# A four-layer graph network on one core: layer-0 scores by symmetry, layer 1 by seven products, and a plan with two times per layer

## The chip, the cores and the metric

The kernel runs on one core of a Trainium2 chip. The metric is the device time in microseconds of one execution; three runs of the kernel before gave 2713.51, 2717.15 and 2717.57 us, so the median is 2717.15 us. The core has five engines with instruction queues of their own: TensorE (PE in the profile, its weight loads PEld), VectorE (DVE), ScalarE (ACT), GpSimd (POOL) and SyncE (SP, which here issues transfers only). They meet through semaphores.

## The reference

The input is 128 graphs of 128 nodes with 256 features, in fp32, and an integer adjacency of 128x128 per graph. Four layers follow each other, and each is wrapped as `x = layernorm(x + layer(x))`:

```python
# layer 0: four scores by edge type, masked, softmax
e_k = leaky_relu(einsum('bid,bjd->bij', hidden * a_k, hidden))   # k = 0..3
alpha = where(adj == k + 1, e_k, ...);  out = softmax(alpha) @ hidden
# layer 1: message sum, mean by in-degree, relu
h = x @ W_msg; msg = einsum('bij,biu->bju', adj, h) / max(deg, 1)
out = relu(x @ W_upd + msg + bias)
# layer 2: three GRU steps with aggregation over adj != 0
m = h @ weight[i]; aggr = einsum('bst,bsd->btd', A, m); h = gru_cell(aggr, h)
# layer 3: graph attention
e = leaky_relu(f_i + f_j), masked by adj > 0; out = elu(softmax(e) @ (h @ W))
```

Two facts are used below. The score of layer 0 before its mask, `(h * a_k) h^T`, is symmetric in i and j. And layer 1 multiplies the same `x` by two square matrices, `W_upd` and `W_msg`, which the kernel holds side by side in `w_um`.

## The kernel before

Graphs go in 32 groups of four (`G = 4`). One group passes `loading`, `layer0`, `layer1`, three `step`s of `gru`, and `layer3`. Features lie in two chunks of 128 (`KC = 2`). Some six groups are in flight at a time.

Nothing is issued while the layers' functions run. Each call is recorded as an `Op` (class at line 156) with the buffers that it reads and writes; every call goes through line 232, so the profile gives nearly all instructions that line, and they are told apart by tile names. At the end a list scheduler (from line 1010 on) walks through a simulated time, in which each engine takes, among the operations that could start, the one with the smallest nominal time, and issues it. That fixes the order of every queue. Nominal times come from `paced(stage, part, g)` at line 338: all operations recorded since the last call are spread evenly, by cost, between two times of the table `TIMES`, moved by `g * PERIOD` and, for the first and last six groups, by the tables `HEAD` and `TAIL`. Durations in the simulation come from cost functions at lines 251 to 287, such as this one for TensorE:

```python
took = 0.11 if op == "transpose" else 0.056 if split else 0.005 + m_of(out[0]) / 600.0
```

Tiles with the same tag share a fixed number of buffers (`hT` has 8, `xb` 2, `xs` 2, `z` 4, PSUM banks `ps` 4 and `gate` 4). For some groups a tag borrows the memory of another (`LENT`, line 973).

**Layer 0** (line 604). `xT` holds the four graphs' features turned over. For each of the four edge types, `prepared(k)` makes a mask `mk` on POOL and two scaled copies `xs` on ACT. TensorE then fills one bank of 512 columns: per graph and feature chunk one matmul, with `xT` as stationary and 128 columns of `xs` moving. DVE copies the bank into `alpha` where the mask is set. Softmax, the product with `x_in`, the residual and the norm follow; the result `xa` is turned over through DRAM into `x1T`.

**Layer 1** (line 669). Per graph, TensorE multiplies `x1T` with all 512 columns of `w_um`, two matmuls. ACT copies the message half into `hu`, whose last column is 1 for the degree, set each time by a POOL memset; DVE adds the bias to the update half. Then one product with the adjacency per graph gives message sums and degree.

**Gates of the GRU** (line 767) already use a scheme of seven products in place of eight. Four 256-column halves live in two banks, and a running sum in `shared` is copied out ("snapshot") at three points between products, each of which makes TensorE wait for the copy before it may add to that bank again. The scheme's sums of inputs are made in `sums`, those of the weights in `weights`.

**Transfers.** A 128x128 turn is a DVE transpose of 32x32 blocks into `z`, a write to DRAM (`way`), and four reads back (`back`, line 506), all issued by SP in order.

Of the kernel before, what the change touches and what calls it, by code (L numbers as in the profile page):

```python
# [8 lines left out]
F32 = mybir.dt.float32  # L9
U8 = mybir.dt.uint8  # L10
# [3 lines left out]
OP = mybir.AluOpType  # L14
# [4 lines left out]
def kernel(  # L19
# [223 lines left out]
    def service(out, ins):  # L243

        tag = out[0].buf.tag if out else "out"
        return 1.5 if tag == "out" else SERVED.get(tag, 0.82 if tag[:3] == "way" else 0.5)
# [39 lines left out]
    def sp_cost(op, n, out, ins, pointers, sums):  # L286
# [10 lines left out]
    PERIOD = 81.73028  # L297
    EAGER, RUSH = 4.9441, 1.5064
    HOP, PE_HOP, SLACK, DMA_SLACK = 0.0975, 0.1022, 0.2622, 0.8243
    STAGES = ("loading", "layer0", "layer1", "step0", "step1", "step2", "layer3")  # L300
    TIMES = {
        "weights": ((-80.6792, -53.8982), (-234.5413, -66.3537), (-85.3398, -177.0436), (-97.3878, -222.0278), (-90.3491, -54.1657), (-171.8955, -44.6841), (-116.1849, 18.7475),),
        "loading": ((-270.5681, -253.3431), (-73.2168, -291.6634),),
        "layer0": ((-167.8607, -107.2636),),
        "layer1": ((-55.0836, 1.9826),),
        "step0": ((-0.0120, 6.9518), (0.2402, 27.6105), (15.5871, 41.1624),),
        "step1": ((50.3003, 61.9650), (57.0688, 76.7749), (63.5441, 96.9672),),
        "step2": ((105.0974, 124.9583), (122.1936, 130.3892), (118.2271, 151.0122),),
        "layer3": ((180.2686, 241.7351),),
    }  # L310
    HEAD = (
        (-8.812, -175.978, -47.271, -14.819, 0.990, 29.605, 4.780),
        (9.303, 38.059, -27.415, 8.695, 4.650, -13.814, 31.463),
        (-161.158, -14.643, 11.133, 0.523, -1.844, 22.264, 10.467),
        (-173.643, 45.499, 14.505, 11.786, 0.810, 10.190, -5.124),
        (-171.750, -3.449, 12.137, -8.917, 5.023, 2.080, 7.957),
        (-245.977, -21.192, 24.177, 5.969, 4.162, 11.377, 24.028),
    )
    TAIL = (
        (127.197, -10.789, 1.076, -13.469, 10.703, 11.032, 13.210),  # L320
        (17.815, -18.016, -1.019, -11.707, 1.115, -15.520, -14.882),
        (80.227, -2.934, 25.075, -16.097, -14.182, 5.595, 38.386),
        (92.761, -52.578, -27.642, -24.660, -19.396, -6.316, 54.637),
        (216.288, -67.705, -36.885, -29.712, 25.798, 36.675, 75.653),
        (364.741, 17.401, 10.112, 11.988, 17.448, 68.637, 12.013),
# [36 lines left out]
    neg_half = tile_of("neg_half", [P, G])  # L362
    acol = tile_of("acol", [P, 4, KC])
# [10 lines left out]

    w_sh = tile_of("w_sh", [P, 3, 3, P])
    w_sm = tile_of("w_sm", [P, NL, 3, 3, P])

    def weights():
# [3 lines left out]
        for src, tag, bufs in ((w_ih, "hT", 8), (w_hh, "rest", 4)):  # L382
# [45 lines left out]
        for i in range(NL):  # L428
            wT = tile_of("hT", [P, KC, D], 8)
# [40 lines left out]


# [132 lines left out]
    def layer0(g, s):  # L604
# [12 lines left out]
        def prepared(k):  # L617
            mk = tile_of("mk", [P, G, N], 2, U8)
            POOL.tensor_scalar(mk, a_f, float(k + 1), None, op0=OP.is_equal)
            xs = []  # L620
            for c in range(KC):
                t = tile_of("xs", [P, T], 2)
                ACT.mul(t, xT[c], acol[:, k, c : c + 1])
                xs.append(t)
            return mk, xs

        ready = [prepared(0)]
        for k in range(4):
            if k < 3:
                ready.append(prepared(k + 1))  # L630
            mk, xs = ready.pop(0)
            ps = bank()
            with PE:
                PE.needs(mk)
                for b in range(G):
                    cols = slice(b * N, (b + 1) * N)
                    for c in range(KC):
                        PE.matmul(ps[:, cols], xT[c][:, cols], xs[c][:, cols], start=(c == 0), stop=(c == KC - 1))
            DVE.copy_predicated(alpha.rearrange(FLAT), mk.rearrange(FLAT), ps)

        leaky(alpha, alpha, 0.0)
        pT, rinv = softmax(alpha, "0", g == 0)
# [26 lines left out]
    def layer1(g, s):  # L669
# [5 lines left out]
        DVE.tensor_scalar(s.a_ne, a_f, 0.0, None, op0=OP.not_equal)  # L675
        hu = []
        for b in range(G):
            hu.append(tile_of("hu", [P, 2 * D + 1], 2))
            POOL.memset(hu[b][:, 2 * D :], 1.0)
            ps = bank()  # L680
            with PE:
                for c in range(KC):
                    PE.matmul(ps, xT[:, b, c, :], w_um[:, c, :], start=(c == 0), stop=(c == KC - 1))
            ACT.copy(hu[b][:, D : 2 * D], ps[:, D:])
            DVE.tensor_add(hu[b][:, :D], ps[:, :D], bias_row)
        res = tile_of("xb", [P, G, D], 2)
# [18 lines left out]
        for c in range(KC):  # L705
            t = tile_of("hT", [P, T], 8)
# [12 lines left out]
    def gru(g, s):  # L719
# [5 lines left out]
        def step(i, hT, parts):  # L725
# [107 lines left out]
            def update(c, z, n, d):  # L833

                DVE.scalar_tensor_tensor(d, z, 1.0, d, op0=OP.add, op1=OP.mult)
                new[c] = n if last_step else tile_of("hT", [P, T], 8)
# [56 lines left out]
    def layer3(g, s, first, last):  # L893
# [50 lines left out]

        res = tile("xd", [P, n, D])
        ninv = tile_of(f"ninv_{three}", [P, n], 2)
        DVE.tensor_scalar_mul(ninv, rinv, -1.0)
        for h in range(n // 2):
# [27 lines left out]
            "probT_0": ("probT_3", 1), "x1T": ("xd", 1), "xs": ("rT", 2),  # L976
        },
        NG - 2: {"xc": ("xa", 2), "rT": ("xT", 2)},
        NG - 1: {
            "q": ("x_in", 1), "t_r": ("x_blocks", 1), "t_i": ("xb", 2), "t_z": ("xb", 2),  # L980
            "xc": ("xa", 2), "rT": ("xs", 2),
        },
    }
# [150 lines left out]
```

## Time and profile before

| What | Value |
|---|---|
| Median of three runs | 2717.15 us |
| The profiled execution | 2713.67 us |
| Its span, first to last instruction | 2711.9 us |
| Mean granted TensorE clock | 0.997 |
| PE busy | 2663.1 us (98%) |
| PE weight loads busy | 2232.4 us (82%) |
| DVE busy | 2187.9 us (81%) |
| ACT busy | 1806.7 us (67%) |
| POOL busy | 1596.5 us (59%) |
| DMA packets | 1317391, 286.89 MB |
| Share of 16 DMA engines, main queue | 50.7% |

An fp32 matmul shows as two records (two matmul records and two weight loads), a bf16 one as one. In the groups by line, layer 0's products `ps<-xs,xT` have 1984 records, layer 1's `ps<-w_um,x1T` 496, and the gates 8064; a few records of layers 0 and 1 stand under other names where a tag borrows memory. Matmul records overlap, since the end of one is modelled past the start of the next; the pace is read from starts. The busy share is an average over stages. `L232` is the recording helper's line, common to nearly all instructions.

### The profile page before, as it was taken

How to read it: one execution, taken by the hardware profiler on the slowest of the kernel's cores; microseconds unless marked ns; L12 is line 12 of the kernel's file. 1: busy time of each engine (PE TensorE's matmuls, PEld its weight loads, DVE VectorE, ACT ScalarE, POOL GpSimd, SP SyncE). 2: the span in 40 equal slices, each digit the busy share in tenths (PEclk: the TensorE clock that was granted, in tenths of full speed). 3: DMA queues.
4: the chain of work that ended last, by engine and by line, in shares of the span. 5: the costliest groups of instructions: out<-in, count | busy, mean ns of one | idle time of the engine just before them, and what ended most of it. 6: DMA issues, size and time to landing. Idle time of an engine off the chain costs nothing.

```text
span 2711.9 us, 45196 instructions
## 1 busy us (share of the span) xinstructions
PE 2663.1 (98%) x14340; PEld 2232.4 (82%) x14340; DVE 2187.9 (81%) x5058; ACT 1806.7 (67%) x4330; POOL 1596.5 (59%) x1538
## 2 busy tenths in 40 slices
PE   8999999999999999999999999999999999999996
PEld 6788888888887888888888888888888888888785
DVE  5777888778788887788887888887888888878877
ACT  4556776666776666766667766767767666667666
POOL 4554576654666555666556665556575555665552
PEclk9999999999999999999999999999999999999999
DMA  5535645554555455555555555555555556435441
GB/s 130 106 78 102 126 91 123 108 104 97 114 113 114 98 121 102 110 113 117 101 117 104 106 117 112 110 113 103 107 116 107 114 113 125 97 75 105 90 86 47
DMA packets 1317391, 286.89 MB, mean 106 GB/s; under 512 B 1068192, under 2 KB 1313056, under 8 KB 1317152
## 3 DMA queue, kind: packets, MB, share of 16 engines
q1 hardware_dynamic: 1314704, 281.63, 50.7%
q8 instruction: 115, 1.88, 0.3%
q10 hardware_dynamic: 2448, 2.36, 0.3%
q14 instruction: 124, 1.02, 0.1%
HBM read 168.44 MB, written 115.41 MB: 105 GB/s over the span
## 4 chain that ended last, share of the span: by engine, by line
PE 85%; DVE 9%; ACT 2%; DMA 2%; issue 1%; SPq 1%; POOL 0%; POOLq 0%; DVEq 0%; ACTq 0%
PE gate L232 58%; PE ps L232 27%; DVE z L232 1%; DVE xb L232 1%; DVE st L232 1%; DVE t_d L232 1%; SPq L232 1%; DVE rest L232 1%; DMA e<-way_f 1%; DVE t_m L232 1%; DVE t_r L232 0%; DVE xa L232 0%; DVE hT L232 0%; DMA hn<-way_h 0%; DVE t_z L232 0%
## 5 line engine op out<-in xcount | busy, mean ns | idle before, releaser
L232 POOL TENSOR_TENSOR t_r<-t_r,t_i 128x512 f32<-128x512 f32 x186 | 244.5, 1322 | 248.9 <-ACT t_i L232 164.4
L232 PE MATMUL gate<-t_h,w_hhT 128*128 128x256 f32 x1152 | 345.8, 383 | 5.1 <-ACT xb L232 2.5
L232 PE MATMUL gate<-t_m,w_sm 128*128 128x256 f32 x1152 | 342.4, 380 | 1.1 <-DVE t_m L232 0.8
L232 PE MATMUL gate<-t_m,c_gi 128*128 128x256 f32 x1152 | 341.8, 379 | 0.0
L232 PE MATMUL gate<-t_h,w_sh 128*128 128x256 f32 x1152 | 339.5, 382 | 1.8 <-ACT q L232 0.9
L232 PE MATMUL gate<-agT,c_gi 128*128 128x256 f32 x1152 | 336.1, 380 | 0.7 <-ACT t_r L232 0.6
L232 PE MATMUL gate<-hT,w_hhT 128*128 128x256 f32 x1152 | 333.7, 381 | 0.2 <-PE gate L232 0.2
L232 POOL TENSOR_TENSOR t_d<-hT,t_n 128x512 f32<-128x512 f32 x192 | 257.3, 1348 | 32.6 <-ACT t_n L232 32.1
L232 POOL TENSOR_TENSOR rstd<-rstd,neg_half 128x4 f32<-128x4 f32 x128 | 147.7, 1154 | 197.6 <-DVE rstd L232 124.7
L232 PEld LDWEIGHTS gate<-t_h,w_hhT 128*128 128x128 f32 x1152 | 208.9, 190 | 60.4 <-issue 23.2
L232 PEld LDWEIGHTS gate<-t_h,w_sh 128*128 128x128 f32 x1152 | 212.3, 190 | 54.3 <-issue 16.7
L232 PEld LDWEIGHTS ps<-xs,xT 128*128 128x128 f32 x1984 | 242.0, 193 | 12.5 <-issue 2.2
L232 PE MATMUL ps<-xs,xT 128*128 128x128 f32 x1984 | 244.2, 276 | 2.6 <-DVE xa L232 1.4
L232 PEld LDWEIGHTS gate<-t_m,w_sm 128*128 128x128 f32 x1152 | 217.1, 190 | 34.1 <-DVE t_m L232 2.2
L232 PEld LDWEIGHTS gate<-agT,c_gi 128*128 128x128 f32 x1152 | 216.8, 190 | 31.8 <-ACT t_r L232 1.2
L232 PEld LDWEIGHTS gate<-t_m,c_gi 128*128 128x128 f32 x1152 | 218.0, 190 | 30.2 <-ACT t_i L232 0.2
L232 PEld LDWEIGHTS gate<-hT,w_hhT 128*128 128x128 f32 x1152 | 214.2, 190 | 30.8 <-issue 2.9
L232 PE MATMUL ps<-w_um,x1T 128*128 128x512 f32 x496 | 232.7, 593 | 1.1 <-ACT x1T L232 1.1
L232 ACT ACTIVATE q<-gate,bhn 128x256 f32<-128x256 f32 x372 | 177.0, 476 | 81.3 <-PE gate L232 77.0
L232 POOL TENSOR_SCALAR mk<-a_f 128x512 uint8<-128x512 f32 x128 | 212.3, 1665 | 20.7 <-DVE alpha L232 13.2
L232 POOL MEMSET alpha<- 128x512 f32 (+1 forms) x63 | 33.1, 525 | 314.0 <-DVE z L232 277.8
L232 ACT ACTIVATE xs<-xT,acol 128x512 f32<-128x512 f32 x248 | 173.2, 719 | 41.2 <-PE ps L232 30.6
(231 smaller groups left out, 6668.0 us busy)
## 6 DMA issues: line engine op xcount, KB each, us to landing
way<-z SPq DMA_DIRECT2D x188, 256.0 KB, 2.4
way_h<-z SPq DMA_DIRECT2D x126, 256.0 KB, 2.4
hn<-way_h SPq DMA_DIRECT2D x504, 64.0 KB, 2.5
x_blocks<-in_x_dram SPq DMA_DIRECT2D x248, 64.0 KB, 2.5
x_in<-in_x_dram SPq DMA_DIRECT2D x31, 512.0 KB, 4.2
way_p<-z SPq DMA_DIRECT2D x62, 256.0 KB, 2.5
probT<-way_p SPq DMA_DIRECT2D x248, 64.0 KB, 2.8
hT<-way SPq DMA_DIRECT2D x248, 64.0 KB, 2.5
```

Of the source, the lines that this page charges most:

```text
L232: getattr(self.engine, name)(*[a.real() if isinstance(a, View) else a for a in args], **{k: a.real() if isinstance(a, View) else a for k, ...
```

## The change

**Layer 0** now handles edge types in pairs. For a pair, `prepared` makes both masks and one tile per feature chunk that holds, for each graph, left and right half of the nodes, and in each half the copies scaled for both types. Group 0 computes as before (`whole`). The other 31 groups use `mirrored`: one product gives the 64 right columns of both types for all 128 rows (128 moving columns); a second one gives the upper left corner of both types, with `xs` as a 128-column stationary and 64 columns of `xT` moving. The lower left block is the upper right one turned over: DVE transposes it in 32x32 blocks, and four SP transfers from SBUF to SBUF put the blocks into place in `left`; ACT copies the corners out, and the second type's corner needs a fifth transfer to reach its partitions. Four predicated copies of 64 columns per graph, two for each half, then fill `alpha`.

**Layer 1** treats two graphs as the halves of the data, `W_upd` and `W_msg` as the halves of the weights. Four sums of data (POOL) and of weights (DVE, once, into `w_ul` and `w_um`) replace eight products of 256 columns by seven, with snapshots between them. The degree column of `hu` is set once for two fixed tiles.

**The plan**: layers 0, 1 and 3 get two pairs of times each, the one boundary inside the layer; all times, the period (81.73 to 79.29) and the constants of waits are new. `hT` goes from 8 to 6 buffers, `xb` from 2 to 1, `mk` from 2 to 4; group 1's and the last group's loans change.

```diff
-    PERIOD = 81.73028
+    PERIOD = 79.28682
...
-            t = tile_of("hT", [P, T], 8)
+            t = tile_of("hT", [P, T], 6)
...
+        b11, b12, b21, b22 = [w_um[:, k, e : e + D] for k in range(KC) for e in (0, D)]
+        DVE.tensor_sub(w_ul[:, 0], b12, b11)
+        DVE.tensor_sub(w_ul[:, 1], b22, w_ul[:, 0])
+        DVE.tensor_sub(w_ul[:, 2], b22, b12)
+        DVE.tensor_sub(b12, b21, w_ul[:, 1])
...
+                t = tile_of("xs", [P, G, 2, 2, H], 2)
+                for k in range(2):
+                    ACT.mul(
+                        t[:, :, :, k], xT[c].rearrange("p (b h n) -> p b h n", [P, G, 2, H], b=G, h=2),
+                        acol[:, 2 * pair + k, c : c + 1],
+                    )
...
+        def mirrored(masks, xs):
+
+            right, corner = bank(), bank()
+            left = tile_of("left", [P, G, 2, H])
+            with PE:
+                PE.needs(*masks)
+                for b in range(G):
+                    for c in range(KC):
+                        PE.matmul(
+                            right[:, b * N : (b + 1) * N], xT[c][:, b * N : (b + 1) * N],
+                            xs[c][:, b, 1].rearrange("p k n -> p (k n)"), start=(c == 0), stop=(c == KC - 1),
+                        )
+            z = tile_of("z", [P, G * 2, H], 4)
+            DVE.transpose(z[:H].rearrange("p m n -> p (m n)"), right[:H])
+            with PE:
+                for b in range(G):
+                    for c in range(KC):
+                        PE.matmul(
+                            corner[:, b * H : (b + 1) * H], xs[c][:, b, 0].rearrange("p k n -> p (k n)"),
+                            xT[c][:, b * N : b * N + H], start=(c == 0), stop=(c == KC - 1),
+                        )
+            corners = corner[:, : G * H].rearrange("p (b n) -> p b n", [P, G, H], b=G)
+            ACT.copy(z[H:, :G], corners[H:])
+            ACT.copy(left[:H, :, 0], corners[:H])
+            rows = left.rearrange("p b k n -> p (b k) n", [P, G * 2, H])
+            for i in range(2):
+                for j in range(2):
+                    SP.dma_start(
+                        out=rows[H + 32 * j : H + 32 * j + 32, :, 32 * i : 32 * i + 32],
+                        in_=z[32 * i : 32 * i + 32, :, 32 * j : 32 * j + 32],
+                    )
+            SP.dma_start(out=left[:H, :, 1], in_=z[H:, :G])
+            for k in range(2):
+                DVE.copy_predicated(
+                    alpha[:, :, H:], masks[k][:, :, H:], right.rearrange("p (b k n) -> p b k n", [P, G, 2, H], b=G, k=2)[:, :, k]
+                )
+            for k in range(2):
+                DVE.copy_predicated(alpha[:, :, :H], masks[k][:, :, :H], left[:, :, k])
...
+        t = tile_of("xd", [P, 2, 3, N])
+        pairs = xT.rearrange("p (h j) c n -> p h j c n", [P, 2, 2, KC, N], j=2)
+        a11, a12, a21, a22 = [pairs[:, :, j, c] for j in range(2) for c in range(KC)]
+        POOL.tensor_add(t[:, :, 0], a21, a22)
+        POOL.tensor_sub(t[:, :, 1], t[:, :, 0], a11)
+        POOL.tensor_sub(t[:, :, 2], a12, t[:, :, 1])
+        POOL.tensor_sub(a21, a11, a21)
...
+            product(sums, xT[:, 2 * h, 0, :], w_um[:, 0, :D], first=True)
+            snapshot(DVE.tensor_add, one[:, :D], sums, bias_row)
+            product(shared[:, D:], xT[:, 2 * h, 1, :], w_um[:, 1, :D], last=True)
+            product(sums, t[:, h, 1], w_ul[:, 1])
+            snapshot(ACT.copy, one[:, D : 2 * D], sums)
+            DVE.tensor_add(one[:, :D], one[:, :D], shared[:, D:])
+            product(other[:, :D], t[:, h, 0], w_ul[:, 0], first=True)
+            product(sums, xT[:, 2 * h + 1, 0, :], w_ul[:, 2])
+            snapshot(ACT.copy, two[:, D : 2 * D], sums)
+            DVE.tensor_add(two[:, D : 2 * D], two[:, D : 2 * D], other[:, :D])
+            product(sums, xT[:, 2 * h + 1, 1, :], w_um[:, 0, D:], last=True)
+            DVE.tensor_add(two[:, :D], sums, bias_row)
+            product(other[:, :D], t[:, h, 2], w_um[:, 1, D:], last=True)
+            DVE.tensor_add(one[:, D : 2 * D], one[:, D : 2 * D], other[:, :D])
+        paced("layer1", 0, g)
+        res = tile_of("xb", [P, G, D], 1)
```

## Prediction

> **What bounds the kernel now.** I began with the table of busy times by engine. It says how full each engine is, not what each stage is worth.
>
> ```profile
> PE 2663.1 (98%) x14340; PEld 2232.4 (82%) x14340; DVE 2187.9 (81%) x5058; ACT 1806.7 (67%) x4330; POOL 1596.5 (59%) x1538
> ```
>
> TensorE (PE) lacks only 49 us of the 2711.9 us span. The busy times by stretch show where these are: 15 us in the first 200, 10 us in the 2300 after that, 21 us in the last 72. In the middle there is nothing to win but matmul time itself:
>
> ```profile
> 1000.00:2000.00 1000.00, 998.65 (x5416) 845.17 (x5415) 826.62 (x1921) 688.53 (x1648) 611.83 (x585) 1.00 0.54 110
> ```
>
> (The columns after the length are PE, weight loads, DVE, ACT, POOL; then clock, DMA share, GB/s.) So the question is how long TensorE takes for a layer-0 or layer-1 product. The groups by line have only overlapping durations (a record of 276 ns is followed by the next after 111), so I took the chain of work in order of time, whose merged pieces give the real pace:
>
> ```profile
> 1300.91 1.78 PE ps L232 x16
> ...
> 1302.69 2.59 PE gate L232 x12
> ...
> 1306.15 0.86 PE gate L232 x4
> ...
> 1352.90 1.72 PE ps L232 x4
> ...
> 1374.18 0.67 PE ps L232 x12
> 1374.86 0.92 PE gate L232 x4
> ```
>
> An fp32 matmul is two records, each with a weight load of its own. The pace of one record is 0.111 us for layer 0's 128 columns (x16), 0.216 us for 256 columns (gates), 0.430 us for layer 1's 512 (1.72 for 4), 0.056 us for a bf16 record of 128 columns. An fp32 record streams its columns twice: 256 to 512 columns costs 0.214 us more, so 128 columns cost 0.107 us of streaming, and 64 would cost 0.054.
>
> The last two lines decide this prediction. The four gate records right after the bf16 ones take 0.92 us, where four others take 0.86. The extra 0.06 us is there whenever fp32 follows bf16: the fp32 weight load begins when the bf16 record before it begins, that record covers 0.056 us of it, and about 0.056 us stand bare. So an fp32 weight load takes some 0.11 us. A second place says it again, after a stall of TensorE:
>
> ```profile
> 1322.91 0.70 PE L232 MATMUL gate<-t_h,w_sh 128*128 128x256 f32 x2 [0.31 <-ACT q L232]
> 1323.44 0.59 PE L232 MATMUL gate<-hT,w_hhT 128*128 128x256 f32 x2
> ```
>
> These two records hold TensorE for 0.53 us (1322.91 to 1323.44) instead of 0.43: with nothing to hide behind, the first load costs 0.10.
>
> **What the Trainium skill says.** "TensorE: Matmul & The Clock Gate", section on LDWEIGHTS, prices a load at columns / 1.2 ns: an estimate of 107 ns for 128 columns. The trace agrees (0.10 bare after the stall, 0.056 + 0.056 after bf16). The same page, section on weight-path performance modes, says the fast load is not had for fp32; the trace agrees, its fp32 load records are 190 ns long and its bf16 ones 98. The same page, Part 2, says that the next weights load while the current matmul streams; the trace agrees, gates run at 0.216 with a load in each. "DMA: Bandwidth & Descriptors", section on why small descriptors are slow, says SBUF to SBUF transfers are spared that penalty; no transfer of this trace goes from SBUF to SBUF.
>
> **The change part by part. Layer 0 on TensorE.** Per graph group, four masks of 16 records are 64 x 0.111 = 7.1 us now. Afterwards (31 groups of 32; group 0 keeps whole products) a pair of masks takes 16 records of 128 columns, 1.78 us, and 16 corner records of 64 columns, each with a fresh 128-column fp32 stationary (`xs[c][:, b, 0]`). If the loads were hidden, a corner record would take 0.054 + 0.002 = 0.056 us, a pair 1.78 + 0.89, and a group would save 2 x 0.89 = 1.78 us, 55 us over 31 groups. If the load binds, a corner record takes 0.111 us, as one of 128 columns, and the group saves nothing. I take nothing: only one load is ahead at a time in this trace (each starts 2 ns after the record before starts), and 64 columns cover half of it. Ends kept: 0 and -55.
>
> **Layer 1 on TensorE.** 16 records x 0.430 = 6.88 us become 2 x 7 x 2 = 28 records x 0.216 = 6.05 us. Here a load (0.11) lies beneath 0.216. Saved: 0.83 us a group, x 32 = **-26.6 us**. This lies wholly on the bounding engine.
>
> **New hand-offs.** Each `shared` bank now goes PE, snapshot, PE three times, six per group, 192 in all. The gates have the same pattern 3 x 384 = 1152 times, and idle before gate matmuls, over their eight groups of rows, sums to 13.8 us, 0.012 us each. So +2.3 us; with a fuller DVE perhaps +8. I take **+3**.
>
> **DVE.** Mirrored layer 0: two transposes of 512 from PSUM at 0.70 (the rows of 128x512 have 0.68 to 0.70; half the partitions I take at the same time, half at the least) = 1.40; eight predicated copies of 256 in place of four of 512. A tensor add goes from 0.680 to 0.415 when halved, so 0.728 becomes about 0.463: 3.70 against 2.91. Together +2.2. Layer 1: ten operations of 256 in place of four, 6 x 0.41 = +2.46. Sum 4.7 us a group, 31 x 2.2 + 32 x 2.46 = 147 us: 2188 becomes about 2335. In the middle a group now takes 81.7 us (the spacing of its layer-1 products), DVE 67.6 of it; later 72.3 of some 80.9, 89%. It hides beneath TensorE, and is the thinnest cover here.
>
> **ACT, POOL, SP.** ACT keeps eight multiplications of 512 and four layer-1 copies; four corner copies of 256 at 0.37 add 1.5 us (69% to 71%). POOL keeps its masks, loses four memsets of 0.1, gains four sums of 256 at 0.80 to 0.93: +3.1 us (61% to 65%). Both hide beneath TensorE. SP issues ten more transfers a group, 310 in all, at 0.49 us each on its queue (its pieces in the chain): 152 us on about 1130 (some 2300 issues now). They wait for DVE's transposed `z` and ACT's copy. Behind them on SP stand the reads that bring `hn` and `hT` back, 2.5 us each, and behind those the next GRU step's split and aggregation. SP already waits 495 us for `z`, so it has room; a delayed `hn` would show up as TensorE idle before `a_ne` products, 3.5 us now. Landing I take as 2.5 us, between 2.0 and 4 by the DMA rows. The lowered buffer counts (`hT` 8 to 6, `xb` 2 to 1) and the shared `xd` act only through the order, 0 with the hand-off's upper end as bound. Setup: four subtractions of 0.41, hidden beneath the first group's work, bare at most 1.7.
>
> **The order.** All queues are re-ordered, with new times for first and last groups. The 36 us idle at the ends can shrink or grow; I take 0, -10 to +10. The plan prices a corner matmul at 0.005 + 64/600 = 0.112 us, two records, where I expect 0.222. Sixteen per group put TensorE 1.8 us behind its plan in each period, so the other engines run ahead of it. From its period of 79.29 us this gives 79.29 + 1.76 = 81.05 against 81.73, -0.7 a group, -21 us over 31: a second route to nearly the same sum.
>
> **Sum.** -26.6 + 0 + 3 = -23.6 us. Profiled execution 2713.67 (span 2711.9 and 1.8 around it) becomes 2690; the median of the runs shown is 3.5 above that execution, so 2717.15 - 23.6 = **2693.5 us**, 0.9% faster.
>
> **Rivals.** *Load binds, layer 1 alone pays* (0.70): 2693.5; its own range is 2680 to 2707, by ends -10 to +10 and hand-offs to +8. *Corner loads hidden* (0.08): 2693.5 - 55 = 2638. For it: no 64-column fp32 record exists here to refute it, and the plan's period of 79.29 fits it. Against: 0.92 against 0.86. *DVE late at the hand-offs, slower* (0.15): at 89% DVE, its snapshots and sums come late to the bank that the next product writes. With 1344 such hand-offs, 0.018 us more on each eats the 24 us, which is the deciding point; at 0.04 more, still short beside a DVE operation of 0.41, it costs 54 us: 2747. For it: ACT waits in `t_z` and DVE waits in `t_r` already alternate in every gate. Against: DVE at 83% leaves only 0.009 us per hand-off between 200 and 2500 us (8.6 us of waits before gates over some 1000), and TensorE late to its plan gives slack. *Gain given back at the ends or to buffers* (0.07): 2717.
>
> **How the numbers follow.** This kernel's runs differ by 0.15%, so 0.2% (5.4 us) counts as a change. Faster 0.77 (0.70 + 0.08, less 0.01 for a likeliest case that ends late), same 0.07, slower 0.16 (0.15 and that 0.01). The range 2655 to 2730 holds the likeliest, no change, the mild slow cases and loads that are half hidden; outside are fully hidden loads and a badly late DVE, under 0.2 together.
>
> **What would show it.** In the changed profile: corner records (64 columns) paced at 0.11, 16 in about 1.78 us, not 0.89; layer-1 records 28 a group at 0.216; DVE near 2335 busy; a period near 80.9 between layer-1 products; idle before gate matmuls still about 14 us. The prediction is wrong if corner records come every 0.056 us, or if TensorE's idle, 49 us, grows by over 24.

## The result and the profile after

The changed kernel is slower: 2760.27 us median (2759.92 to 2761.90), against 2716.84 us for the kernel before on the same chip. The ratio is 1.0163, with a 95% interval of 1.0146 to 1.0181. The forecast was 2693.5 us, with a range of 2655 to 2730.

The profiled execution has a span of 2758.1 us (before 2711.9). Its table of busy times by engine answers to the first line of the prediction:

```profile
PE 2670.9 (97%) x14724; PEld 2301.4 (83%) x14724; DVE 2299.1 (83%) x5440; ACT 1841.6 (67%) x4454; POOL 1697.9 (62%) x1540
```

TensorE still bounds the kernel, but the busy share fell while the span grew: 87 us are idle where 49 were. The busy times by stretch (length, then PE, weight loads, DVE, ACT, POOL; clock, DMA share, GB/s) say where. First two stretches of the kernel before, then the same two after:

```profile
0.00:200.00 200.00, 185.07 (x990) 147.02 (x991) 138.76 (x342) 103.54 (x231) 104.15 (x114) 0.99 0.49 105
200.00:2500.00 2300.00, 2290.02 (x12393) 1928.84 (x12392) 1882.20 (x4345) 1567.62 (x3770) 1396.87 (x1339) 1.00 0.53 109
```

```profile
0.00:200.00 200.00, 174.78 (x933) 143.70 (x934) 141.48 (x348) 97.79 (x224) 95.80 (x98) 0.94 0.50 103
200.00:2500.00 2300.00, 2264.38 (x12572) 1963.39 (x12571) 1953.22 (x4620) 1577.86 (x3821) 1477.69 (x1332) 1.00 0.56 113
```

And the thousand from the middle, after:

```profile
1000.00:2000.00 1000.00, 994.06 (x5554) 868.03 (x5553) 852.34 (x2038) 698.40 (x1695) 636.79 (x583) 1.00 0.56 114
```

In the first 200 us 25 are idle (15 before), in the next 2300 it is 36 (10 before), and in the thousand from the middle 5.9 (1.35 before).

The timeline of TensorE (start, duration, then the operation, with the count of records) shows layer 0's new pair of products:

```profile
1328.24 1.95 PE L232 MATMUL ps<-xs,xT 128*128 128x128 f32 x16
1330.03 1.90 PE L232 MATMUL ps<-xT,xs 128*128 128x64 f32 x16
1331.76 0.65 PE L232 MATMUL gate<-hT,w_sh 128*128 128x256 f32 x2
1332.25 1.03 PE L232 MATMUL gate<-agT,w_sm 128*128 128x256 f32 x4
```

Sixteen records of 128 columns hold TensorE for 1.79 us (1328.24 to 1330.03), and sixteen corner records of 64 columns for 1.73 (to 1331.76). The two gate records behind them take 0.49 instead of 0.43: that is the bare load of an fp32 weight again, 0.06, which a short record doesn't cover. With it the corners hold TensorE for the same 1.79 us, at half the columns.

The same view near the start, where the first group has layer 1 almost to itself, shows the new hand-offs bare (the bracket is idle time before the piece, and what ended it):

```profile
65.88 0.76 PE L232 MATMUL ps<-w_um,x1T 128*128 128x256 f32 x2
66.47 0.59 PE L232 MATMUL ps<-w_ul,xd 128*128 128x256 f32 x2
67.97 0.70 PE L232 MATMUL ps<-w_um,x1T 128*128 128x256 f32 x2 [0.90 <-DVE hu L232]
68.51 0.59 PE L232 MATMUL ps<-w_ul,xd 128*128 128x256 f32 x2
70.02 0.70 PE L232 MATMUL ps<-w_ul,x1T 128*128 128x256 f32 x2 [0.92 <-DVE hu L232]
71.18 0.70 PE L232 MATMUL ps<-w_um,x1T 128*128 128x256 f32 x2 [0.46 <-ACT hu L232]
```

Three waits of half a microsecond to one, each with a copy of 0.37 or a sum of 0.41 in it. In the middle of the kernel, other groups' matmuls stand between these products and cover most of this.

The groups by line, shapes apart (busy, mean ns | idle before, and what ended it), show two gate groups, the corners, and layer 1's products that use a bank after a snapshot:

```profile
L232 PE MATMUL gate<-t_h,w_hhT 128*128 128x256 f32 x1152 | 342.6, 384 | 9.9 <-ACT t_z L232 5.8 <-ACT q L232 1.9 <-POOL xd L232 1.2
L232 PE MATMUL gate<-agT,c_gi 128*128 128x256 f32 x1152 | 338.4, 383 | 5.6 <-ACT agT L232 5.5
L232 PE MATMUL ps<-xT,xs 128*128 128x64 f32 x992 | 119.2, 274 | 0.0
L232 PE MATMUL ps<-w_um,x1T 128*128 128x256 f32 x372 | 112.8, 385 | 4.3 <-DVE hu L232 2.3 <-ACT hu L232 2.0
L232 PE MATMUL ps<-w_ul,x1T 128*128 128x256 f32 x124 | 38.0, 389 | 2.5 <-ACT hu L232 1.5 <-DVE hu L232 0.9
```

Idle before gates sums to 34.2 us over the eight gate groups, where it was 13.8, though the change touches no gate.

**An account that the busy share can't give.** A record's end is modelled past the start of the next, so idle time by busy records misses the beginning of every wait. "Perfetto Trace Analysis" of the Trainium skill, section on identifying the most-contended engine, says that the busy share of matmuls is not a good measure of how close a kernel is to its roofline, because pipelined instructions look smaller in a trace. Here they look longer (384 ns at a pace of 216), and the share of 97% hides over a third of the waits. I therefore went by starts. Each record has a pace: 0.112 us for fp32 of 64 or 128 columns, 0.216 for 256, 0.429 for 512, 0.056 for bf16, and 0.056 more for the first fp32 record after bf16 ones. In a run of corners the first takes 0.056 less and the record behind the run 0.056 more, so a run counts as 16 x 0.112. The sum of the paces is TensorE's work. What a record takes beyond its pace, until the next one starts, is a wait, put down to the record that comes late. (By kind, only waits above 0.02 us are counted, so the kinds don't sum exactly.)

| TensorE by starts, us | before | after | difference |
|---|---|---|---|
| work | 2629.1 | 2602.9 | -26.3 |
| waits, all | 66.9 | 139.0 | +72.1 |
| before gates | 33.2 (195 waits) | 73.8 (363) | +40.6 |
| before layer 1's products | 1.3 (2) | 23.5 (77) | +22.2 |
| before all others | 31.8 (97) | 40.8 (126) | +9.0 |
| waits in 0 to 200 / 200 to 2500 / the rest | 21.0 / 27.1 / 18.8 | 38.3 / 76.6 / 24.0 | |

-26.3 + 72.1 = +45.8 us, against a span longer by 46.2. So the whole result is here: the work fell as forecast (26.6), and waits of nearly three times its gain came in.

A part of these waits is the clock. In some stretches the trace grants TensorE half the clock; there a record takes twice its pace, and the excess counts above as a wait. One such stretch of the changed kernel (the clock is the 0.50), and sixteen layer-0 records in it, which hold TensorE for 3.37 us (83.37 to the next record at 86.74) instead of 1.79:

```profile
79.90:86.60 6.70, 5.02 (x24) 4.86 (x25) 6.24 (x15) 4.73 (x9) 6.44 (x6) 0.50 0.28 68
```

```profile
83.37 3.53 PE L232 MATMUL ps<-xs,xT 128*128 128x128 f32 x16
```

Up to 2500 us such stretches sum to 30.7 us, where the kernel before has 3.4. An estimate from the starts in them: 13 of the 139.0 us are excess of this kind, 3 of the 66.9 before. So some 10 of the 72 us of new waits are the clock, most of them in the first 200 us.

### The profile page after: what moved, and what is told of

The parts are those of the page before. It is cut to its first block, busy times and chain, and to the rows that moved or that the text cites. A ratio compares the mean times of both kernels' runs of the same rounds, so it can differ in the third digit from the quotient of the medians.

```text
span 2758.1 us, 46926 instructions
## 1 busy us (share of the span) xinstructions
PE 2670.9 (97%) x14724; PEld 2301.4 (83%) x14724; DVE 2299.1 (83%) x5440; ACT 1841.6 (67%) x4454; POOL 1697.9 (62%) x1540
## 4 chain that ended last, share of the span: by engine, by line
PE 75%; DVE 12%; ACT 8%; issue 2%; POOL 1%; DMA 1%; SPq 1%; DVEq 0%; POOLq 0%; ACTq 0%
PE gate L232 52%; PE ps L232 23%; ACT xd L232 2%; ACT t_z L232 2%; DVE t_d L232 1%; ACT t_n L232 1%; DVE z L232 1%; DVE st L232 1%; DVE shift L232 1%; DVE alpha L232 1%; DVE t_m L232 1%; DVE hT L232 1%; DVE t_z L232 1%; ACT agT L232 1%; DVE xb L232 1%
## 5 line engine op out<-in xcount | busy, mean ns | idle before, releaser
L232 POOL TENSOR_TENSOR rstd<-rstd,neg_half 128x4 f32<-128x4 f32 x128 | 155.6, 1216 | 292.5 <-DVE rstd L232 276.3
L232 ACT COPY t_i<-gate 128x256 f32<-128x256 f32 x372 | 137.8, 371 | 112.6 <-PE gate L232 108.8
L232 ACT COPY t_z<-gate 128x256 f32<-128x256 f32 x288 | 106.3, 369 | 153.8 <-PE gate L232 152.2
L232 ACT COPY t_r<-gate 128x256 f32<-128x256 f32 x279 | 104.1, 373 | 126.6 <-PE gate L232 125.5
L232 DVE TENSOR_TENSOR t_z<-gate,t_z 128x256 f32<-128x256 f32 x192 | 105.5, 550 | 97.3 <-PE gate L232 68.0
```

What stands on the lines that cost most here:

```text
L232: getattr(self.engine, name)(*[a.real() if isinstance(a, View) else a for a in args], **{k: a.real() if isinstance(a, View) else a for k, ...
```

## The experiments

Two explanations stood at the start. One is the prediction's slower rival: DVE, fuller now, comes late at the hand-offs. The other is the order of the queues: the plan was made anew, and TensorE waits because of where the work stands in it. Within the second there is the under-priced corner (55 us that the plan doesn't know of). Where an expectation speaks of A and B, A is the first and B the second.

### Shorter pieces of the changed kernel, its order kept

In `corner_half` the corner products leave out the second chunk of features, half of their records:

```diff
             with PE:
                 for b in range(G):
                     for c in range(KC):
                         PE.matmul(
                            corner[:, b * H : (b + 1) * H], xs[c][:, b, 0].rearrange("p k n -> p (k n)"),
                            xT[c][:, b * N : b * N + H], start=(c == 0), stop=(c == KC - 1),
                        )
+            ops[-1].calls = [(name, args, dict(kw, stop=True)) for name, args, kw in ops[-1].calls if kw["start"]]
```

> The changed kernel with every queue in the same order, but the corner products use the first feature chunk only: 8 records of 64 columns in place of 16 per pair. That leaves out half of the corner's sum, and takes 62 x 8 x 0.111 = 55 us off TensorE, just what a hidden weight load would have saved. Theory A (DVE comes late at the hand-offs, TensorE waits for it): little of it reaches the end, 2740 to 2756. Theory B (the order was laid out for a TensorE that is faster at the corners, TensorE is the bound all the same and its unpriced time adds in full): 2705, 50 to 58 lower.

In `l1_copies_short` the ten DVE and four ACT operations between layer 1's products are done on 8 of 256 columns:

```diff
-        nc.gpsimd.memset(hu_tile[:, 2 * D :], 1.0)
+        nc.gpsimd.memset(hu_tile, 1.0)
...
-        hu = []
+        hu, mark = [], len(ops)
...
+        for op in ops[mark:]:
+            if op.engine in (DVE, ACT):
+                op.calls = [(name, tuple(v[:, :8] for v in args), kw) for name, args, kw in op.calls]
```

> The changed kernel with every queue in the same order, but the ten DVE and four ACT operations between layer 1's seven products handle 8 columns of 256, so most of hu keeps its first value. DVE loses some 10 x 0.25 us a group (80 us), ACT 4 x 0.2, and each wait of TensorE for a snapshot is 0.2 to 0.25 us shorter. A: DVE's load is what is late, so 30 us or more go: below 2730. B: only what TensorE waits before layer 1's products goes, some 20 us of bare time in the trace: 2740 to 2750.

In `l0_masked_short` layer 0's four predicated copies of a pair are done on 8 of 64 columns:

```diff
+            for op in ops[-4:]:
+                op.calls = [(name, tuple(v[:, :, :8] for v in args), kw) for name, args, kw in op.calls]
```

> The changed kernel with every queue in the same order, but the predicated copies that end a mirrored pair (four of 256 per pair) handle 8 of 64 columns per graph, so most scores stay masked. DVE loses about 8 x 0.29 us a group, 72 us. A: 20 us or more lower, below 2740. B: within 8 us of the changed kernel.

In `before_dve_twice` the kernel before, in its own order, does layer 0's predicated copies and layer 1's bias sums twice:

```diff
                 DVE.copy_predicated(alpha, masks, ps)
+                ops[-1].calls *= 2
...
             DVE.tensor_add(hu[b][:, :D], ps[:, :D], bias_row)
+            ops[-1].calls *= 2
```

> The kernel before with every queue in the same order, but layer 0's four predicated copies and layer 1's four bias sums are issued twice: DVE gains 4 x 0.73 + 4 x 0.41 = 4.6 us a group, 146 us, about what the change adds, at the same places. A: 30 us or more slower than before, above 2747. B: within 12 us of before.

| | median, us | ratio to before | TensorE's work / waits, us |
|---|---|---|---|
| corner_half | 2721.69 | 1.0028 [1.0018, 1.0038] | 2547.5 / 152.4 |
| l1_copies_short | 2744.16 | 1.0108 [1.0093, 1.0123] | 2602.9 / 124.4 |
| l0_masked_short | 2753.85 | 1.0144 [1.0127, 1.0161] | 2602.9 / 133.0 |
| before_dve_twice | 2781.38 | 1.0243 [1.0228, 1.0258] | 2629.1 / 133.7 |

Halving the corner records takes 55.4 us of work off TensorE and 37 off the time (0.0163 - 0.0028 of 2715; differences between kernels are taken from ratios in this way). Waits rise by 13. So corners do cost what records of 128 columns cost, but nothing says that the plan's ignorance of them makes the waits: with the plan's price met, the waits are larger. Both expectations were missed, B's 2705 and A's 2740 to 2756.

Layer 1's shorter copies give back 15 us, 8 of them before layer 1's own products (23.5 to 15.5), 7 before gates. Layer 0's copies give 5, while waits before gates fall by 6 (73.8 to 67.7): DVE's work there is well covered. Both came out as B said.

The last run is a warning. DVE's busy time in it is like that of the changed kernel:

```profile
PE 2695.2 (97%) x14340; PEld 2230.5 (80%) x14340; DVE 2317.8 (83%) x5314; ACT 1797.0 (65%) x4330; POOL 1588.8 (57%) x1538
```

130 us more on DVE (2317.8 - 2187.9) cost 66 us, with gates waiting 80.5 instead of 33.2. So DVE work put where the order has no room for it is not hidden by an average of 83%. That is what A said, and it spoke for the DVE rival. The next runs asked whether it holds for the changed kernel.

### The changed plan with the old arithmetic

`neither_new_plan` keeps the changed plan (times, period, constants, buffers) and computes as before: layer 0 whole for all groups, layer 1 with 512 columns (only `hu`'s degree column is still set once). `seven_new_plan` puts back layer 0 only, and `mirrored_new_plan` layer 1 only.

```diff
-            if g == 0:
-                whole(*ready[pair])
-            else:
-                mirrored(*ready[pair])
+            whole(*ready[pair])
...
-            product(sums, xT[:, 2 * h, 0, :], w_um[:, 0, :D], first=True)
...
+                    PE.matmul(ps, xT[:, b, c, :], w_um[:, c, :], start=(c == 0), stop=(c == KC - 1))
```

> The changed kernel with both layers' arithmetic put back (whole products in layer 0 for all groups, eight products in layer 1), laid out anew by the changed plan's times, constants and buffer counts. Theory B (the plan's order itself holds TensorE): the plan's own simulation ends at 2705.5 us here, 2676.3 for the kernel before; the chip's span stood 36 us above that before, so 2705.5 + 36 + 4 = 2746. Theory A (DVE's added work is the loss): it is as the kernel before, 2717 within 10.

> The changed kernel with layer 0's products whole for all groups, layer 1 by seven products, laid out anew by the changed plan. B: the simulation ends at 2754.2, TensorE priced rightly, so 2754 + 40 = 2794. A: DVE loses 2.2 us a group against the changed kernel and TensorE's work is the same: 2735 to 2750, and near 2693 if layer 0 was all of the loss.

> The changed kernel with layer 1 by eight products, layer 0 mirrored, laid out anew by the changed plan. B: the simulation ends at 2699.9, and 55 us of corner time are unpriced: 2700 + 40 + 55 = 2795. A: TensorE has 26.6 us more and DVE 2.5 us a group less than in the changed kernel: 2745 to 2765.

| | median, us | ratio to before | work / waits | waits before gates, layer 1, others |
|---|---|---|---|---|
| neither_new_plan | 2760.22 | 1.0173 [1.0156, 1.0190] | 2630.2 / 111.8 | 73.9, 0.1, 37.3 |
| seven_new_plan | 2810.94 | 1.0358 [1.0343, 1.0374] | 2603.5 / 190.2 | 116.8, 18.8, 53.8 |
| mirrored_new_plan | 2802.13 | 1.0324 [1.0309, 1.0340] | 2629.8 / 152.2 | 92.3, 4.1, 55.1 |

The first line is the turning point of the study. These lines of `neither_new_plan` are from its busy times by engine and its groups by line:

```profile
PE 2682.8 (97%) x14340; PEld 2227.5 (81%) x14340; DVE 2195.9 (80%) x5058; ACT 1792.6 (65%) x4330; POOL 1581.4 (57%) x1412
```

```profile
L232 PE MATMUL gate<-t_h,w_hhT 128*128 128x256 f32 x1152 | 348.3, 386 | 16.2 <-ACT t_z L232 8.6 <-POOL xd L232 1.7 <-ACT q L232 1.6
```

TensorE and DVE have the instructions of the kernel before, to the number (14340 and 5058), and DVE is busy for 2195.9 us, about as then (2187.9). Yet the kernel is as slow as the changed one, and gates wait 73.9 us, as in the changed one (73.8). So the waits before gates need neither the extra DVE work nor the new hand-offs: this order has them without either. A's 2717 is out; B's 2746 was 14 us short. (For the other two B was 17 and 7 us short, and A further off.)

Two runs that keep the changed kernel's own order say the same of DVE. `l0_masked_short` takes DVE's busy time from 2299.1 to 2244.9 us, and `l1_copies_gone`, which follows below, to 2223.3; of the 73.8 us before gates, 67.7 and 67.0 stay. If the two add up, DVE's load makes some 13 of the 40.6 us of new waits there. A late DVE is refuted as the main cause of them.

It also says what the new arithmetic does within this plan. From `neither_new_plan` to the changed kernel, work falls by 27.3 (2630.2 to 2602.9) and waits rise by 27.2, 23.4 of them before layer 1's products. The hand-offs eat most of what seven products save.

One doubt stays with these three kernels. The changed times were made for both parts together, so each partial kernel runs in times that don't fit it; seven_new_plan and mirrored_new_plan are each worse than both and neither. So the equal 73.9 and 73.8 may be luck in part, and these kernels can't price a part of the change. For that each version needs times of its own.

### Times searched anew

For four arithmetics I searched period, times, head, tail and the planner's two weights (`EAGER`, `RUSH`) in the kernel's own planner, with the constants of waits of the kernel before, the changed kernel's buffer counts, and TensorE priced as the traces have it:

```diff
-        took = 0.11 if op == "transpose" else 0.056 if split else 0.005 + m_of(out[0]) / 600.0
+        took = 0.11 if op == "transpose" else 0.056 if split else max(0.2235, 0.005 + m_of(out[0]) / 600.0)
...
-    PERIOD = 79.28682
+    PERIOD = 80.445966
...
-        "layer0": ((-167.7835, -129.8118), (-130.3586, -106.8765),),
...
```

(The period shown is that of the arithmetic before; 0.056 more is priced for the first fp32 product after bf16. The record holds the times found, not how long each search ran.)

> The arithmetic of the kernel before with the changed kernel's buffer counts, the plan's times searched anew, with TensorE priced as the trace has it (0.2235 us for an fp32 matmul of 128 columns or fewer, 0.056 more for the first fp32 one after bf16). Its simulation ends at 2690.8; that of the kernel before, priced so, at 2716.9, where the chip's span was 2711.9. Theory O (the order is what was lost, the buffers are not): 2690 to 2715, 45 us or more below the same arithmetic under the changed plan (2760). Theory F (the fewer buffers cost it): above 2740.

> Layer 0 mirrored, layer 1 by eight products, times searched anew with the same prices; its simulation ends at 2695.1. O: within 12 us of neither_replanned, since corner loads leave TensorE's work as it was and DVE's 2.2 us a group are hidden. S (what the new arithmetic adds on DVE and SP cannot be hidden in any order): 20 us or more above neither_replanned.

> Layer 0 whole, layer 1 by seven products, times searched anew with the same prices; its simulation ends at 2702.9, with 20 us of TensorE idle left between 2000 and 2400 us and 39 in the first 200. O: the middle stretch runs at 80.6 to 81.0 us a group, 0.8 below neither_replanned, and the whole at 2695 to 2720. S: the middle stretch stays at 81.7 or more.

> The changed kernel's arithmetic, times searched anew with the same prices; its simulation ends at 2690.8, where the changed plan priced so ends at 2876 and priced as it was at 2660. O: 2690 to 2715, 45 us or more below the changed kernel, the middle stretch at 80.6 to 81.2 us a group. S: above 2735.

| | planner's end, us | median, us | ratio to before | work / waits | waits before gates, layer 1, others |
|---|---|---|---|---|---|
| neither_replanned | 2690.8 | 2729.36 | 1.0056 [1.0041, 1.0071] | 2628.9 / 82.0 | 39.9, 1.9, 39.7 |
| mirrored_replanned | 2695.1 | 2738.98 | 1.0091 [1.0076, 1.0106] | 2630.3 / 89.9 | 52.0, 1.3, 35.9 |
| seven_replanned | 2702.9 | 2742.99 | 1.0111 [1.0096, 1.0126] | 2603.4 / 121.5 | 48.4, 28.0, 44.5 |
| both_replanned | 2690.8 | 2730.89 | 1.0057 [1.0040, 1.0074] | 2603.8 / 110.4 | 51.8, 17.6, 40.2 |

`both_replanned` does the changed kernel's arithmetic, with its buffers, in another order, and is 29 us faster (1.0163 - 1.0057, of 2715). Its stretches:

```profile
0.00:200.00 200.00, 174.76 (x909) 142.66 (x910) 136.44 (x325) 96.75 (x222) 95.24 (x97) 0.93 0.49 102
200.00:2500.00 2300.00, 2284.23 (x12745) 1988.21 (x12744) 1998.87 (x4696) 1588.11 (x3862) 1499.31 (x1341) 1.00 0.56 113
```

TensorE is idle for 16 us of the middle 2300 instead of 36, with DVE fuller than in the changed kernel (1998.87 against 1953.22). By starts, waits in the middle fall from 76.6 to 47.0, and those before gates from 73.8 to 51.8. So some 29 of the 44 us are the order that this plan makes, and not the arithmetic. `neither_replanned` against `neither_new_plan` says the same of the old arithmetic: 32 us (1.0173 - 1.0056). It has the changed buffer counts too, so these cost at most the 15 us that it still lies above the kernel before; that part may as well be the search.

Of the expectations, O was right in direction and too high in size: three of the four kernels missed its range, by 14 to 23 us, and the gain over the changed plan was 29 to 32 us, not 45. In the middle the groups follow each other at 81.7 us in `both_replanned` and 81.9 in `seven_replanned` (median spacing of layer 1's first products), where O had said at most 81.2 and 81.0; for `seven_replanned` that is what S said. F and S missed their times. Only `mirrored_replanned` came out as O said.

Among the four searched orders, no new part gains. Mirrored layer 0 alone costs 9.5 us: it saves TensorE nothing and adds work for DVE, ACT and SP. Seven products alone have 25.5 us less work and 39.5 us more of waits, two thirds of them (28.0 - 1.9) in front of layer 1's own products. The next experiments asked where these stand.

### The hand-offs themselves, and leaving out the head's

In `l1_copies_gone` the same DVE and ACT operations between layer 1's products are left out, with the order of all else kept, so no product waits for a snapshot (`mark` and `hu`'s first value as in `l1_copies_short`):

```diff
+        for op in ops[mark:]:
+            if op.engine in (DVE, ACT):
+                op.calls = []
```

> The changed kernel with every queue in the same order, but the ten DVE and four ACT operations between layer 1's seven products left out, so that hu keeps its first value and TensorE has no hand-off there. Theory H (the hand-offs, not DVE's load, eat layer 1's gain): the 23.5 us that TensorE stands before layer 1's products in the changed kernel fall below 5, and the time by 20 to 32 us, to 2728 to 2740. Theory D (the load on DVE and ACT delays the gates): the time falls by 40 us or more, the 74 us before gate products with it, since DVE loses 4.1 us a group.

It took 2735.81 us, 1.0076 [1.0059, 1.0092], or 24 us less than the changed kernel, as H said. These are its groups for layer 1's products:

```profile
L232 PE MATMUL ps<-w_um,x1T 128*128 128x256 f32 x372 | 110.9, 380 | 0.0
L232 PE MATMUL ps<-w_ul,x1T 128*128 128x256 f32 x124 | 37.2, 382 | 0.0
```

By starts, waits before layer 1's products fall from 23.5 to 2.5 us, those before gates only from 73.8 to 67.0. D is out. So the hand-offs cost some 21 us directly. Of the 23.5 us, 13.7 lie in the first 200 us (an estimated 2.3 of them half clock), where few groups are in flight and the waits stand bare as in the timeline above; 9.4 lie in the next 2300. Hence the last version: layer 0 whole everywhere, layer 1 by eight products for the first four groups and by seven for the other 28, with times searched anew. `late_seven_b` has the same arithmetic in a second searched order, with the same planned end of 2668.9.

```diff
-    w_ul = tile_of("w_ul", [P, 3, D])
+    w_ul = tile_of("w_ul", [P, 4, D])
...
-        DVE.tensor_sub(b12, b21, w_ul[:, 1])
+        DVE.tensor_sub(w_ul[:, 3], b21, w_ul[:, 1])
...
-            if g == 0:
-                whole(*ready[pair])
-            else:
-                mirrored(*ready[pair])
+            whole(*ready[pair])
...
+        if g < 4:
+            hu = []
+            for b in range(G):
+                hu.append(tile_of("hu", [P, 2 * D + 1], 2))
+                ps = bank()
+                with PE:
+                    for c in range(KC):
+                        PE.matmul(ps, xT[:, b, c, :], w_um[:, c, :], start=(c == 0), stop=(c == KC - 1))
+                ACT.copy(hu[b][:, D : 2 * D], ps[:, D:])
+                DVE.tensor_add(hu[b][:, :D], ps[:, :D], bias_row)
+        else:
...
```

> Layer 0 whole for all groups; layer 1 by eight products for the first four groups and by seven for the other 28; times searched anew with the trace's prices, its simulation ends at 2668.9. The four replanned kernels ran 37 to 42 us above their simulations. H: the hand-offs stand bare mostly where few groups overlap (11 to 17 of 18 to 28 us in the first 200), so this keeps 28 x 0.83 = 23 us less some 8: 2700 to 2722, 10 to 25 us below neither_replanned (2729). D: no better than neither_replanned.

> The same arithmetic as late_seven_a with another order from the search, whose simulation also ends at 2668.9. H: 2700 to 2722, and within 10 us of late_seven_a, so that the difference is not one order's luck. D: no better than 2729.

| | median, us | ratio to before | work / waits | waits before gates, layer 1, others |
|---|---|---|---|---|
| late_seven_a | 2705.80 | 0.9971 [0.9960, 0.9981] | 2607.2 / 80.1 | 44.4, 5.0, 30.2 |
| late_seven_b | 2716.62 | 1.0012 [1.0005, 1.0019] | 2607.2 / 91.3 | 51.4, 7.0, 32.0 |

`late_seven_a` beats both kernels: 8 us below the kernel before, 52 below the changed one. Its busy times by engine, and its first two stretches:

```profile
PE 2644.4 (98%) x14676; PEld 2294.2 (85%) x14676; DVE 2253.3 (83%) x5230; ACT 1799.1 (67%) x4330; POOL 1683.3 (62%) x1524
```

```profile
0.00:200.00 200.00, 187.00 (x1016) 148.97 (x1017) 147.69 (x339) 105.11 (x237) 106.34 (x102) 1.00 0.48 102
200.00:2500.00 2300.00, 2278.40 (x12743) 1994.82 (x12742) 1948.53 (x4541) 1563.02 (x3774) 1482.97 (x1338) 1.00 0.53 109
```

13 us are idle in the first 200 (25 in the changed kernel), with DVE just as full over the whole (83%) and the clock at 1.00 (0.94). Against `neither_replanned`, searched in the same way, work is 21.7 us less and waits are 1.9 less: the whole gain of seven products arrives (23 us by the ratios). `late_seven_b` keeps half of it. Both lie in H's range, but the two orders, equal in the plan, are 11 us apart on the chip, more than the 10 that H allowed. So a difference of ten between two searched orders can be luck, and the gain of seven products that two orders show is 12 to 23 us. The step from `seven_replanned`, 38 and 27 us, is larger than that; the 9.5 of mirrored layer 0 is not.

## Why the prediction was wrong, step by step

**Corner records.** Right, the mechanism too; layer 0 saves TensorE nothing. The prediction chose this end by its 0.92 us against 0.86, and the rival of hidden loads (2638) is out. The starts show a hidden and a bare load side by side. The first corner of a run, whose load lies beneath the longer record ahead, takes 0.056 us (59 of 62 runs), the prediction's figure for a hidden load. From the second on each takes 0.112 (915 of 930; the other 15, at 0.213, stand in half-clock stretches). The record behind the run takes 0.056 more. In all that is 16 x 0.112. "TensorE: Matmul & The Clock Gate" of the Trainium skill, section on LDWEIGHTS, from which the prediction estimated 107 ns for a load, agrees: with 64 columns it is the load that sets the pace.

**Layer 1.** Right: 28 records at 0.216. TensorE's work fell by 26.3, the forecast was 26.6.

**New hand-offs, "I take +3".** Mis-sized by seven times. Waits before layer 1's products are 23.5 us, 0.122 for each of 192, not 0.012. The price was the mean over the gates, which stand in the middle of the kernel with some six groups in flight; at the head the bare hand-offs shown cost 0.46 to 0.92 each, and 13.7 us of the sum lie there. Even in the middle, 9.4 us is three times the +3. The price was also taken from idle time between busy records, 13.8 us before gates, where starts give 33.2.

**"The order: I take 0, -10 to +10."** This is the step that failed: the new order was put at nothing. The changed plan costs about 47 us with the arithmetic of before (its buffer counts and the misfit of its times included), and 29 of the changed kernel's 44 go when another order is searched for the same arithmetic. The prediction looked only at the ends (36 us of idle time there), and took the plan's period as a time that the plan keeps: "79.29 + 1.76 = 81.05". The period is only the spacing of due times. The measured spacing of groups in the middle (median, by layer 1's first products) went from 81.7 to 82.1. The sign that the prediction had named came: TensorE's idle time grew by 38 us, from 49 to 87. The planner, run by itself, shows as much: it ends at 2676.3 before and at 2660.1 after, 16 us earlier, while the work that it prices for TensorE falls by 79.3 (2615.3 to 2536.0). So 63 us more of TensorE's waits stand in its own order. The chip shows 72.1 more; since the plan prices the corners 55 us too low, these are not the same waits one by one.

**DVE.** The work added was nearly right: 78.7 us in layer 1 (192 sums of 0.410), and 72 in layer 0. Two lines show where its prices were off, in opposite directions:

```profile
L232 DVE COPY_PREDICATED alpha<-mk,left 128x256 f32<-128x256 uint8 x120 | 64.2, 535 | 1.8 <-DMA left<-z 1.7
L232 DVE COPY_PREDICATED alpha<-mk,ps 128x256 f32<-128x256 uint8 x120 | 50.6, 422 | 2.6
```

0.463 was taken for both. (The 535 is a mean with a long tail, see the end.) DVE's busy time rose by 111 us to 2299.1, not by 147; the 40 us between that and the work added is spread over other groups of rows, and I didn't follow it. That DVE hides it "beneath TensorE" holds if the order makes room for it: `late_seven_a` at 83% does, `before_dve_twice` at 83% doesn't.

**SP and transfers.** 310 issues took 0.65 us each instead of 0.49, and landed in 2.0 to 2.2 us instead of 2.5. The tell-tale that was named, TensorE idle before `a_ne` products, stayed small: 3.5 us before, 2.5 after (0.2, 0.6 and 1.7 in the three groups by line).

**The rivals.** "DVE late at the hand-offs" came nearest in time (2747) and by its sign: gates wait 0.035 us more per hand-off (40.6 / 1152), near its 0.04. But it had the wrong cause in the main, since these waits are there with DVE's load as before, and taking DVE's new work away leaves most of them. It named one true thing, that hand-offs are the thinnest place. "Gain given back at the ends or to buffers" let waits eat only the gain, where they ate nearly three times as much, and had their place wrong: 49.5 of the 72.1 us of new waits lie between 200 and 2500 us.

**What stays open.** Which of the plan's numbers makes the order bad was not separated, nor why the changed kernel's clock is halved more often. The four searched orders ran 39 to 44 us above their planned ends, the last two 37 and 48, while the kernel before, with TensorE priced in the same way, has a planned end of 2716.9 and a span of 2711.9: its order is better than the planner's prices can tell, and I found no reason.

## What to carry to other kernels

When a change moves the order of every queue, the order is a term of the sum with a size of its own. Running the old arithmetic under the new plan, and the new arithmetic under another plan, brackets it (47 and 29 us here), and a period written in a plan is no evidence that the plan keeps it. In this kernel a product that must wait for a copy of its own bank costs, on the mean, 0.03 to 0.06 us where other groups' matmuls stand between (33.2 / 1152 for the gates before, 9.4 / 168 for layer 1 between 200 and 2500 us), and half a microsecond to one where none do. So use a scheme with fewer products where groups overlap and the plain one at the head. Halving the columns of fp32 matmuls with fresh weights paid from 256 to 128 (0.216 to 0.112 us a record) and not from 128 to 64 (0.112 again), where the load sets the pace.

## What the hardware showed beyond expectation

- Predicated copies of 256 elements per partition take 535 ns on the mean with their data in SBUF (`left`) and 422 with them in PSUM (the 512 of before took 728 from PSUM). The medians, the second figure of the three here, are close together; only the copies from SBUF have a long tail:

```profile
L232 DVE COPY_PREDICATED alpha<-mk,left x120: 397/444/1533, 90.4 to 2546.2; 128x256 f32<-128x256 uint8 x120
L232 DVE COPY_PREDICATED alpha<-mk,ps x124: 395/424/735, 22.9 to 2527.5; 128x256 f32<-128x256 uint8 x120, 128x512 f32<-128x512 uint8 x4
```

  Of the 120 from SBUF, 55 ran with POOL idle nearly throughout (median 440 ns) and 19 with POOL busy nearly throughout (844); those from PSUM don't differ (431 and 416). No run took POOL's work away, so this is a coincidence in time and not a cause shown.
- A DVE transpose of 512 elements takes as long on 64 partitions as on 128, 705 ns in this group of the changed kernel where those of 128x512 have means of 678 to 699:

```profile
L232 DVE STREAM_TRANSPOSE z<-ps 64x512 f32<-64x512 f32 x62 | 43.7, 705 | 22.2 <-PE ps L232 20.8 <-DMA hT<-way 1.0
```

- Idle time between busy matmul records hides about the first 0.17 us of every wait behind a 256-column record (384 ns long, the next can start after 216), so 87 us of idle time stood for 139 us of waits.
